# A two-layer graph kernel: the first batch's epilogue by halves and in another order, and the last head's columns finished as a half and two quarters

## The chip, the cores and the metric

The kernel runs on one core of one Trainium2 chip. The time is the device time of the whole program in microseconds (us), the median of several executions. All data is float32. The engines are called PE (TensorE), DVE (VectorE), ACT (ScalarE), POOL (GpSimd) and SP (SyncE, which issues most of the transfers). Each takes its own instructions in program order, and semaphores connect them.

## The reference, cut to what matters

There are 16 graphs (batches) of 1024 nodes with 128 features. Each goes through two layers, and each layer ends in a residual and a layernorm.

```python
# layer 0
h = x @ Ww + Wb
e = (h @ A) @ h.T;  e = e + e.T                        # symmetric scores, 1024 x 1024
attention = softmax(where(adj > 0, e, 0), axis=1) * adj
h_prime = relu(attention @ h)
ic, fc, oc = (sigmoid(h_prime @ w_u + x @ w_x) for three pairs of vectors)
x = layernorm(x + oc * tanh(ic * h_prime + fc * x))
# layer 1, four heads
h = x @ conv_w[head] + conv_b[head]
Ah = tanh(adj * (h @ attn_w[head] @ h.T))
x = layernorm(x + relu(relu(mean over heads of relu(Ah @ h)) + x))
```

## The kernel before

**Tiling.** The 1024 nodes are 8 blocks (`NB`) of 128, or two halves (`NH`) of 512 columns. A matmul works on at most 512 columns; in float32 it is two instructions on PE. PSUM has a ring of four small tiles (`ps_sc`, tag `sc`) that every score, projection and transpose shares, and two accumulators of 1024 columns (`ps_acc`, tags `acc0` for layer 0 and `acc1` for layer 1).

**Layer 0 in pieces.** `layer0(b)` returns a dictionary of pieces with one-letter names, and `run` calls them in the order of a string. For batch b: `L` loads xT and the eight adjacency blocks; `X` loads x; `Q0`, `Q1` project the queries (L199); `H` projects h with the gates' columns, three groups of matmuls (`pR_h`, L268), each followed by a DVE addition (L269); `S0` to `S7` are scores of the upper triangle (L283, copied by ACT into R in L286); `T0` to `T6` turn blocks into the lower triangle, by PE transposes for the first batch (L301), by a DVE transpose and transfers through DRAM for all others (L308 to L315); `A` masks, takes maxima and exponentials (L324 to L330); `B` multiplies by the adjacency and scales h (L335 to L339) and then issues the products of the block before (`back`, L347). After these comes the epilogue: `R` (relu, hpT, L356), `P` and `p` (rows of h', L366), `G` (gates, and POOL's product u = x * gate, L378), `I` (L384 and tanh, L388), `O` (L395), then the layernorm in two steps, `V` (statistics on DVE, L182 to L186, and a power on POOL, L187) and `N` (L190). `turn_x1`, `head_uT` and `rows` then prepare layer 1 (L439, L199, L448).

**Layer 1 in steps.** Each batch has 32 steps (4 heads of 8 blocks). `layer1_step` computes the scores of a block (L469), multiplies by the adjacency on DVE (L470), takes tanh on ACT (L471) and pushes the product with h (`back`, L475) onto a queue that runs two steps later (`DELAY`). When a head is done, `sum` takes its relu (L485, L487). Between the steps stand the pieces of the next batch's layer 0, by the list `BETWEEN`; a piece that has already run is skipped. The queries of the batch after that stand at step 31, its loads at step 28, behind `turn_x1` of step 27 on SP's queue.

**The two ends.** For the first batch the order of pieces is written out by hand, mixed with pieces of the second batch and with `join`, four steps that prepare layer 1's weights:

```python
run(first, "... T5 S6 A5 B4")
run(second, "Q0 Q1")
run(first, "T6 S7 A6 B5 A7 B6 B7")
```

The second batch's S0 to S7 and T0 to T2 all run there. At the other end, `layer1_end` of the last batch transposes the sums on PE (L501), adds x1 (L504, L508), runs the layernorm over all eight blocks and stores 512 KB from POOL's queue (L511).

Of the kernel before, what the change touches and what calls it, by code (L numbers as in the profile page):

```python
# [11 lines left out]
F32 = mybir.dt.float32  # L12
AF = mybir.ActivationFunctionType
ALU = mybir.AluOpType
# [3 lines left out]
P = 128  # L18
# [4 lines left out]
def two_layer_adjacency_kernel(  # L23
# [19 lines left out]
    nc = tc.nc  # L43
# [15 lines left out]
    def small(name):  # L59
        return ps_sc.tile([P, 512], F32, tag="sc", name=name)  # L60
# [108 lines left out]
    def push(back):  # L169
        pending.append(back)  # L170
        if len(pending) > DELAY:
            pending.popleft()()

    def layernorm(t, dst, name):

        st = sb.tile([P, NB, nc.vector.BN_STATS_DIM], F32, tag="st", name=f"st_{name}")
        mv = sb.tile([P, NB, 2], F32, tag="mv", name=f"mv_{name}")  # L180
        for k in range(NB):
            nc.vector.bn_stats(st[:, k, :], t[:, k, :])  # L182
        for k in range(NB):
            nc.vector.bn_aggr(mv[:, k, :], st[:, k, :])
        rs = sb.tile([P, NB], F32, tag="rs", name=f"rs_{name}")
        nc.vector.tensor_scalar_add(rs, mv[:, :, 1], EPS)  # L186
        nc.gpsimd.tensor_tensor(rs, rs, mhalf, ALU.pow)  # L187
        yield
        for k in range(NB):
            nc.vector.tensor_scalar(  # L190
                dst[:, k, :], t[:, k, :], mv[:, k, 0:1], rs[:, k : k + 1],
                ALU.subtract, ALU.mult,
            )
# [41 lines left out]
    def layer0(b):  # L235
# [22 lines left out]
                t["qT"] = sb.tile([P, N], F32, tag="qT0", name=f"qT0_{b}", bufs=1)  # L258
            project_T(t["qT"], q_w, t["xT"], c_col, f"q0_{b}", [q])

        def project_h():

            h = t["h"] = sb.tile([P, NB, G], F32, tag="h0", name=f"h0_{b}", bufs=1)
            for ks in GROUPS:
                ps = small(f"pR_h0_{b}_{ks[0]}")[:, : len(ks) * G]
                ps = ps.rearrange("p (k d) -> p k d", d=G)
                for i, k in enumerate(ks):
                    nc.tensor.matmul(ps[:, i, :], t["xT"][:, ts(k, P)], wwT_g, start=True, stop=True)  # L268
                nc.vector.tensor_add(  # L269
                    h[:, ks[0] : ks[-1] + 1, :], ps,  # L270
                    wb_row.unsqueeze(1).to_broadcast([P, len(ks), G]),
                )
            t["gate"] = sb.tile([P, NB, 3], F32, tag="gate", name=f"gate_{b}")
            nc.vector.tensor_copy(t["gate"], h[:, :, D : D + 3])

        def score(j):
            if j == 0:
# [91 lines left out]
        def gates():  # L369

            gate = t["gate"]
            gflat = gate.rearrange("p k g -> p (k g)")
            nc.vector.tensor_add(gate, t["hp"][:, :, D : D + 3], gate)
            nc.scalar.activation(gflat, gflat, AF.Exp, scale=-1.0)
            nc.vector.tensor_scalar_add(gflat, gflat, 1.0)
            nc.vector.reciprocal(gflat, gflat)
            t["u"] = sb.tile([P, NB, D], F32, tag="u", name=f"u0_{b}", bufs=1)
            nc.gpsimd.tensor_mul(t["u"], t["x"], gate[:, :, 1:2].to_broadcast([P, NB, D]))  # L378

        def inner():  # L380
            u, gate, hp = t["u"], t["gate"], t["hp"]
            for q in range(NH):
                for k in range(q * BH, (q + 1) * BH):
                    nc.vector.scalar_tensor_tensor(  # L384
                        u[:, k, :], hp[:, k, :D], gate[:, k, 0:1], u[:, k, :],
                        op0=ALU.mult, op1=ALU.add,
                    )
                nc.scalar.activation(  # L388
                    u[:, q * BH : (q + 1) * BH, :], u[:, q * BH : (q + 1) * BH, :], AF.Tanh
                )  # L390

        def outer():
            u, gate = t["u"], t["gate"]
            for k in range(NB):
                nc.vector.scalar_tensor_tensor(  # L395
                    u[:, k, :], u[:, k, :], gate[:, k, 2:3], t["x"][:, k, :],
                    op0=ALU.mult, op1=ALU.add,
                )

            t["x1"] = sb.tile([P, NB, D + 1], F32, tag="x1", name=f"x1_{b}")  # L400
            nc.gpsimd.memset(t["x1"][:, :, 0:1], 1.0)
            t["norm"] = layernorm(u, t["x1"][:, :, 1 : D + 1], f"0_{b}")

        def finish():
            next(t["norm"], None)
            x1_t[b] = t["x1"]

        pieces = {
            "L": load, "H": project_h, "X": load_x, "R": relu,
            "P": lambda: rows_hp(GROUPS[:-1]), "p": lambda: rows_hp(GROUPS[-1:]),  # L410
            "G": gates, "I": inner, "O": outer, "V": lambda: next(t["norm"]), "N": finish,
        }
        for q in range(NH):
            pieces[f"Q{q}"] = partial(project_q, q)
        for j in range(NB):
# [39 lines left out]
        project_T(uT, ms[:, hd, :], x1T_t[b], None, f"u1_{b}_{hd}")  # L455
        u_t[b, hd] = uT

    acc1_t, sum_t = {}, {}

    def layer1_step(b, hd, m):  # L460
        x1T, h1, uT = x1T_t[b], h1_t[b, m], u_t[b, hd]
        adj = adj_t[b][m]
        if m == 0:
            acc1_t[b, hd] = ps_acc.tile([P, N], F32, tag="acc1", name=f"acc1_{b}_{hd}")
        acc = acc1_t[b, hd]
        s = sb.tile([P, N], F32, tag="s1", name=f"s1_{b}_{hd}_{m}", bufs=4)
        for q in range(NH):
            ps = ps_sc.tile([P, 512], F32, tag="sc", name=f"sc1_{b}_{hd}_{m}_{q}")
            nc.tensor.matmul(ps, x1T[:, ts(m, P)], uT[:, ts(q, 512)], start=True, stop=True)  # L469
            nc.vector.tensor_mul(s[:, ts(q, 512)], ps, adj[:, ts(q, 512)])  # L470
        nc.scalar.activation(s, s, AF.Tanh)  # L471

        def back():
            for q in range(NH):
                nc.tensor.matmul(  # L475
                    acc[:, ts(q, 512)], h1[:, ts(hd, D)], s[:, ts(q, 512)],
                    start=(m == 0), stop=(m == NB - 1),
                )
            if m == NB - 1:
                if hd == 0:  # L480
                    sum_t[b] = sb.tile([P, N], F32, tag="sum", name=f"sum_{b}", bufs=1)
                for q in range(NH):
                    o, a = sum_t[b][:, ts(q, 512)], acc[:, ts(q, 512)]
                    if hd == 0:
                        nc.vector.tensor_scalar_max(o, a, 0.0)  # L485
                    else:
                        nc.vector.scalar_tensor_tensor(o, a, 0.0, o, op0=ALU.max, op1=ALU.add)  # L487

        push(back)

    def layer1_end(b):
        x1 = x1_t[b][:, :, 1 : D + 1]
        y = sb.tile([P, NB, D], F32, tag="u", name=f"y_{b}", bufs=1)
        if b + 1 < B:
            turn(y.rearrange("p k d -> p (k d)"), sum_t[b].rearrange("p (k d) -> p k d", d=P), f"sum_{b}")
            yield
            nc.vector.scalar_tensor_tensor(y, y, 1.0 / H, x1, op0=ALU.mult, op1=ALU.add)
        for q in range(NH if b + 1 == B else 0):
            pt = small(f"pt2_{b}_{q}")
            for i in range(BH):  # L500
                nc.tensor.transpose(pt[:, ts(i, P)], sum_t[b][:, ts(q * BH + i, P)], ident)  # L501
            rows = slice(q * BH, (q + 1) * BH)

            nc.vector.scalar_tensor_tensor(  # L504
                y[:, rows, :], pt.rearrange("p (k d) -> p k d", d=D), 1.0 / H, x1[:, rows, :],
                op0=ALU.mult, op1=ALU.add,
            )
        nc.vector.scalar_tensor_tensor(y, y, 0.0, x1, op0=ALU.max, op1=ALU.add)  # L508
        yield
        yield from layernorm(y, y, f"1_{b}")  # L510
        nc.gpsimd.dma_start(out[b].rearrange("(k p) d -> p k d", p=P), y)  # L511

# [2 lines left out]
    run(first, "L X")  # L517
    load_late_weights()
    run(second, "L")
    run(first, "Q0 H S0 Q1 T0 S1 A0 T1 S2 A1 B0 T2 S3 A2 B1 T3 S4 A3 B2 T4 S5 A4 B3 T5 S6 A5 B4")  # L520
    run(second, "Q0 Q1")
    run(first, "T6 S7 A6 B5 A7 B6 B7")
    next(join)
    run(first, "R")
    run(second, "H")
    run(first, "P p G")
    next(join)
    run(second, "S0 S1 T0")
    next(join)
    run(first, "I")  # L530
    next(join, None)
    run(second, "S2 S3")
    run(first, "O V")
    run(second, "T1 T2 S4 S5 S6 S7")
    run(first, "N")
    turn_x1(0)
    head_uT(0, 0)
    rows(0, range(NB))

    BETWEEN = [
        "H", "S0", "T0 S1", "T1 S2", "T2 A0", "S3 B0", "T3 A1", "S4 B1",
        "T4 A2", "S5 B2", "T5 A3", "S6 B3", "T6 A4", "S7 B4", "A5", "B5",
        "A6", "B6", "A7", "B7", "X R", "P", "p G", "I",
        "O", "V", "N", "", "", "", "", "",
    ]
    AHEAD = {28: "L", 31: "Q0 Q1"}
    TURN = 27
# [23 lines left out]
        end = layer1_end(b)  # L573
    while pending:
        pending.popleft()()
    for _ in end:
        pass


# [37 lines left out]
```

## Time and profile before

| | us |
|---|---|
| median of 3 runs | 2462.53 |
| lowest and highest | 2461.43, 2468.94 |
| the profiled execution | 2458.88 |
| its span, first to last instruction | 2457.1 |
| PE busy | 2427.1 (99%) |
| DVE busy | 1588.5 (65%) |
| ACT busy | 1083.5 (44%) |

The profile is of one execution. In its rows, an arrow `out<-in` names what an instruction writes and reads, L12 is line 12 of the kernel, and a bracket gives the idle time before an instruction and what ended it. The chain that ended last follows the program back from its last instruction: each piece is what released the next one. The table of stretches gives, for each engine, its busy time in a stretch, and then PE's granted clock, where 1.00 is full speed.

### The profile page before, as it was taken

Reading aid. Unit: us, or ns where it says so; the run is one execution under the profiler, and the core shown is the slowest. Engines: PE = TensorE matmul, PEld = TensorE weight load, DVE = VectorE, ACT = ScalarE, POOL = GpSimd, SP = SyncE. Lnnn points to the kernel's source line nnn. Section 1 sums busy time; section 2 is a strip of 40 time slices with the busy share of each in tenths; the row PEclk is TensorE's granted clock in tenths of the full one; section 3 lists DMA queues with packets and bytes.
Section 4 is the critical chain, followed back from the end, with each engine's and each line's share of the span. In section 5 each row is a group of like instructions: output and inputs, shape, how many; then the busy total and the mean of one; then the engine's idle time right before and its main releaser. Section 6 shows DMA issues by size and latency. Waiting matters only on the chain.

```text
span 2457.1 us, 19849 instructions
## 1 busy us (share of the span) xinstructions
PE 2427.1 (99%) x6159; PEld 1118.7 (46%) x6159; DVE 1588.5 (65%) x3010; ACT 1083.5 (44%) x1522; POOL 112.5 (5%) x91
## 2 busy tenths in 40 slices
PE   8999999999999999999999999999999999999997
PEld 4444444444444444444444444444444444444443
DVE  6665848657576565866658576585765848657554
ACT  5544444444444444434444444344444444444432
POOL 0000000000000000000000000000000000000000
PEclk9999999999999999999999999999999999999999
DMA  5204223041240512314033240322304223051000
GB/s 181 51 11 133 55 95 87 8 145 43 95 94 9 147 34 102 87 26 139 25 116 73 68 109 13 123 67 94 84 11 136 53 94 88 7 148 41 23 21 9
DMA packets 408127, 180.75 MB, mean 74 GB/s; under 512 B 352598, under 2 KB 376022, under 8 KB 408023
## 3 DMA queue, kind: packets, MB, share of 16 engines
q1 hardware_dynamic: 404855, 171.11, 25.1%
q0 software_dynamic: 2304, 8.39, 1.2%
q8 instruction: 49, 0.80, 0.1%
q14 instruction: 55, 0.45, 0.1%
q10 hardware_dynamic: 864, 0.00, 0.0%
HBM read 127.80 MB, written 51.64 MB: 73 GB/s over the span
## 4 chain that ended last, share of the span: by engine, by line
PE 96%; DVE 2%; DMA 1%; SPq 0%; ACT 0%; issue 0%; POOL 0%; POOLq 0%; DVEq 0%; ACTq 0%
PE acc L475 35%; PE sc L469 35%; PE acc L347 9%; PE sc L283 5%; PE pT_u L199 4%; PE pR L448 4%; PE pT_q L199 1%; PE pR_h L268 1%; PE pt L366 1%; DMA xT<-in_xT_dram 1%; SPq L228 0%; POOL rs L187 0%; DVE st L182 0%; DMA dram_x<-turn_x 0%; ACT R L330 0%
## 5 line engine op out<-in xcount | busy, mean ns | idle before, releaser
L470 DVE TENSOR_TENSOR s<-sc,adj 128x512 f32<-128x512 f32 x1024 | 682.4, 685 | 640.0 <-PE sc L469 627.1
L475 PE MATMUL acc<-s,h 128*128 128x512 f32 x2048 | 962.0, 592 | 0.0
L469 PE MATMUL sc<-uT,x1T 128*128 128x512 f32 x2048 | 962.0, 592 | 0.0
L471 ACT ACTIVATE s<-s 128x1024 f32<-128x1024 f32 x512 | 541.5, 1058 | 824.9 <-DVE s L470 820.0
L475 PEld LDWEIGHTS acc<-s,h 128*128 128x128 f32 x2048 | 387.7, 190 | 491.2 <-issue 482.1
L469 PEld LDWEIGHTS sc<-uT,x1T 128*128 128x128 f32 x2048 | 385.7, 190 | 468.8 <-issue 423.3
L347 PE MATMUL acc<-R,hz 128*128 128x512 f32 x512 | 243.0, 597 | 4.4 <-ACT hz L339 4.4
L330 ACT ACTIVATE R<-R,nmax 128x1024 f32<-128x1024 f32 x128 | 147.0, 1149 | 207.8 <-DVE nmax L328 196.9
L335 DVE TENSOR_TENSOR R<-R,adj 128x1024 f32<-128x1024 f32 x128 | 156.1, 1219 | 5.4 <-ACT R L330 0.2
L328 DVE TENSOR_REDUCE nmax<-R 128x1 f32<-128x1024 f32 x128 | 156.1, 1220 | 4.4
L324 DVE SCALAR_TENSOR_TENSOR R<-adj,R 128x1024 f32<-128x1024 f32 (+1 forms) x129 | 153.0, 1187 | 3.9 <-PE turn L301 3.9
L347 PEld LDWEIGHTS acc<-R,hz 128*128 128x128 f32 x512 | 95.9, 191 | 113.7 <-issue 87.2
L283 PE MATMUL sc<-xT,qT 128*128 128x512 f32 (+3 forms) x384 | 143.9, 486 | 0.0
L286 ACT ACTIVATE R<-sc,h 128x512 f32<-128x512 f32 (+1 forms) x192 | 108.8, 578 | 38.8 <-PE sc L283 37.2
L199 PE MATMUL pT_u<-x1T,ms 128*128 128x512 f32 x256 | 120.4, 592 | 0.0
L187 POOL TENSOR_TENSOR rs<-rs,mhalf 128x8 f32<-128x8 f32 x32 | 64.6, 2018 | 1211.8 <-DVE rs L186 758.7
L448 PE MATMUL pR<-cw,x1T 128*128 128x512 f32 x256 | 114.9, 592 | 0.0
L339 ACT ACTIVATE hz<-h,rz 128x128 f32<-128x128 f32 x128 | 51.2, 400 | 128.3 <-DVE rz L337 128.1
L283 PEld LDWEIGHTS sc<-xT,qT 128*128 128x128 f32 x384 | 69.7, 190 | 68.8 <-issue 57.0
L451 ACT COPY h<-pR 128x512 f32<-128x512 f32 x128 | 74.9, 585 | 41.9 <-PE pR L448 41.9
L487 DVE SCALAR_TENSOR_TENSOR sum<-acc,sum 128x512 f32<-128x512 f32 x96 | 61.8, 686 | 35.9 <-PE acc L475 35.1
L308 DVE STREAM_TRANSPOSE turn<-R 128x896 f32<-128x896 f32 (+6 forms) x105 | 73.2, 697 | 14.1 <-DMA dram<-turn 11.4
(96 smaller groups left out, 909.4 us busy)
## 6 DMA issues: line engine op xcount, KB each, us to landing
adj<-in_adjT_dram SPq DMA_DIRECT2D x128, 512.0 KB, 7.7
xT<-in_xT_dram SPq DMA_DIRECT2D x16, 512.0 KB, 4.5
x<-in_x_dram SPq DMA_DIRECT2D x16, 512.0 KB, 4.1
out_dram<-y POOLq DMA_DIRECT2D x16, 512.0 KB, 4.0
dram_x<-turn_x SPq DMA_DIRECT2D x15, 512.0 KB, 2.6
x1T<-dram_x SPq DMA_DIRECT2D x60, 128.0 KB, 3.2
dram_sum<-turn_sum SPq DMA_DIRECT2D x15, 512.0 KB, 2.6
y<-dram_sum SPq DMA_DIRECT2D x60, 128.0 KB, 3.1
```

What stands on the lines that cost most here:

```text
L199: nc.tensor.matmul(ps, w, src[:, ts(q, 512)], start=True, stop=True)
L283: nc.tensor.matmul(ps[:, : at - lo], t["qT"][:, ts(j, P)], t["xT"][:, lo:at], start=True, stop=True)
L324: nc.vector.scalar_tensor_tensor(s[:, ks], adj[:, ks], 0.0, s[:, ks], op0=ALU.is_gt, op1=ALU.mult)
L328: nc.vector.tensor_reduce(nmax, s, AX.XY, ALU.max, negate=True)
L330: nc.scalar.activation(s, s, AF.Exp, bias=nmax, accum_out=t["z", j])
L335: nc.vector.tensor_mul(s, s, adj_t[b][j].rearrange("p (k d) -> p k d", d=P))
L347: nc.tensor.matmul(t["acc"][:, ts(q, 512)], t["hz", j], t["R"][:, ts(q, BH), j, :], start=(j == 0), stop=(j == NB - 1),)
L448: nc.tensor.matmul(ps, x1T_t[b][:, ts(k, P)], cw.rearrange("p h d -> p (h d)"), start=True, stop=True)
L469: nc.tensor.matmul(ps, x1T[:, ts(m, P)], uT[:, ts(q, 512)], start=True, stop=True)
L470: nc.vector.tensor_mul(s[:, ts(q, 512)], ps, adj[:, ts(q, 512)])
L471: nc.scalar.activation(s, s, AF.Tanh)
L475: nc.tensor.matmul(acc[:, ts(q, 512)], h1[:, ts(hd, D)], s[:, ts(q, 512)], start=(m == 0), stop=(m == NB - 1),)
```

## The change

In the opening, `H` is divided into its three groups, `H0`, `H1` and `H2`. For the first batch, u, `I`, `O`, `V` and `N` work on two halves of four blocks (`PARTS`); the other batches keep one part. The memset of x1's first column moves from `O` to `G` for all batches. The written order is new: T6 and S7 stand ahead of the second batch's Q0 and Q1, the first batch's `P p G` ahead of the second batch's `H0 H1`, T0 to T2 of the second batch come after the first batch's epilogue, and its S4 to S7 are left to the list `BETWEEN`.

At the end, the last head's tanh results are all kept in one tile (in the buffer of R). Its queue runs the products of columns 0 to 511 alone. Columns 512 to 767 and 768 to 1023 follow as two quarters, each in a PSUM tile of its own (`last_back`), and `last_end` finishes four, two and two blocks with a store from SP each.

```diff
-        st = sb.tile([P, NB, nc.vector.BN_STATS_DIM], F32, tag="st", name=f"st_{name}")
...
+        n = t.shape[1]
+        st = sb.tile([P, n, nc.vector.BN_STATS_DIM], F32, tag="st", name=f"st_{name}")
...
-        nc.gpsimd.tensor_tensor(rs, rs, mhalf, ALU.pow)
+        nc.gpsimd.tensor_tensor(rs, rs, mhalf[:, :n], ALU.pow)
...
-            nc.gpsimd.tensor_mul(t["u"], t["x"], gate[:, :, 1:2].to_broadcast([P, NB, D]))
+            t["x1"] = sb.tile([P, NB, D + 1], F32, tag="x1", name=f"x1_{b}")
+            for ks in PARTS:
+                nc.gpsimd.tensor_mul(
+                    t["u"][:, ks], t["x"][:, ks],
+                    gate[:, ks, 1:2].to_broadcast([P, ks.stop - ks.start, D]),
+                )
+            nc.gpsimd.memset(t["x1"][:, :, 0:1], 1.0)
...
+        PARTS = [slice(0, NB)] if b else [slice(0, BH), slice(BH, NB)]
...
+        last = (b, hd) == (B - 1, H - 1)
+        if last:
+            if m == 0:
+                kept.append(sb.tile([P, NB, N], F32, tag="R", name="kept", bufs=1))
+            s = kept[0][:, m, :]
...
-        push(back)
+        push(partial(back, [0]) if last else back)
...
+    def last_back(acc, ms, at):
+
+        for m in ms:
+            nc.tensor.matmul(
+                acc, h1_t[B - 1, m][:, ts(H - 1, D)], kept[0][:, m, at : at + 256],
+                start=(m == 0), stop=(m == NB - 1),
+            )
+        if ms[-1] == NB - 1:
+            add_head(B - 1, H - 1, acc, at)
...
+    def last_end(b, k0, k1):
+
+        n = k1 - k0
+        x1 = x1_t[b][:, k0:k1, 1 : D + 1]
+        y = sb.tile([P, n, D], F32, tag="s1", name=f"y_{b}_{k0}", bufs=4)
+        pt = small(f"pt2_{b}_{k0}")[:, : n * P]
+        for i in range(n):
+            nc.tensor.transpose(pt[:, ts(i, P)], sum_t[b][:, ts(k0 + i, P)], ident)
+        nc.vector.scalar_tensor_tensor(
+            y, pt.rearrange("p (k d) -> p k d", d=D), 1.0 / H, x1, op0=ALU.mult, op1=ALU.add
+        )
+        nc.vector.scalar_tensor_tensor(y, y, 0.0, x1, op0=ALU.max, op1=ALU.add)
+        yield from layernorm(y, y, f"1_{b}_{k0}")
+        rows = out[b, k0 * P : k1 * P, :]
+        nc.sync.dma_start(rows.rearrange("(k p) d -> p k d", p=P), y)
...
-    run(first, "Q0 H S0 Q1 T0 S1 A0 T1 S2 A1 B0 T2 S3 A2 B1 T3 S4 A3 B2 T4 S5 A4 B3 T5 S6 A5 B4")
-    run(second, "Q0 Q1")
-    run(first, "T6 S7 A6 B5 A7 B6 B7")
+    run(first, "Q0 H0 S0 H1 H2 Q1 T0 S1 A0 T1 S2 A1 B0 T2 S3 A2 B1 T3 S4 A3 B2 T4 S5 A4 B3")
+    run(first, "T5 S6 A5 B4 T6 S7 A6 B5")
+    run(second, "Q0")
+    run(first, "A7 B6")
+    run(second, "Q1")
+    run(first, "B7 R")
     next(join)
-    run(first, "R")
-    run(second, "H")
     run(first, "P p G")
+    run(second, "H0 H1")
     next(join)
-    run(second, "S0 S1 T0")
+    run(second, "S0")
+    run(first, "I0 I1")
+    run(second, "S1")
+    run(first, "O0 V0 O1")
     next(join)
-    run(first, "I")
+    run(second, "H2 S2")
+    run(first, "V1")
     next(join, None)
-    run(second, "S2 S3")
-    run(first, "O V")
-    run(second, "T1 T2 S4 S5 S6 S7")
-    run(first, "N")
+    run(second, "S3")
+    run(first, "N0 N1")
     turn_x1(0)
     head_uT(0, 0)
+    run(second, "T0 T1 T2")
     rows(0, range(NB))
...
-    for _ in end:
-        pass
+    ends = [last_end(B - 1, k, k + n) for k, n in ((0, 4), (4, 2), (6, 2))]
+    for i, at in enumerate((512, 768)):
+        acc = ps_acc.tile([P, N], F32, tag=f"acc{i}", name=f"acc_end_{i}")[:, :256]
+        last_back(acc, range(NB // 2), at)
+        next(ends[i])
+        if i:
+            next(ends[i - 1], None)
+        last_back(acc, range(NB // 2, NB), at)
+    next(ends[2])
+    for e in ends[1:]:
+        next(e, None)
```

## Prediction

> **What bounds the kernel now.** Read the page first: engine shares, then its chain that ended last.
>
> ```profile
> span 2457.1 us, 19849 instructions
> PE 2427.1 (99%) x6159; PEld 1118.7 (46%) x6159; DVE 1588.5 (65%) x3010; ACT 1083.5 (44%) x1522; POOL 112.5 (5%) x91
> PE 96%; DVE 2%; DMA 1%; SPq 0%; ACT 0%; issue 0%; POOL 0%; POOLq 0%; DVEq 0%; ACTq 0%
> ```
>
> PE is the bound. From 69.9 us to 2440.3 its matmuls follow each other at 0.43 us per 512-column instruction, bar some 4 us. So time can be won only before that stretch, where PE starves, and after it, where PE is done and other engines finish. The chain over the first 130 us comes next (columns: start, length, what):
>
> ```profile
> 41.77 3.57 PE acc L347 x4
> 45.35 2.01 PE acc L347 x4
> 47.36 1.05 PE p_last L145 x2
> 48.41 1.92 PE acc L347 x4
> 50.33 1.80 PE pR_h L268 x16
> 52.12 1.79 PE pt L366 x16
> ...
> 56.83 0.59 DVE turn L308
> ...
> 57.86 2.14 DVE u L384 x8
> 60.01 2.10 DVE u L395 x8
> 62.11 1.55 DVE st L182 x8
> ...
> 64.49 1.69 POOL rs L187
> ```
>
> After the first batch's last products (acc) the chain passes through work of the second batch (pR_h, turn) before the first batch's gates and layernorm. The timeline and the table of stretches show what made acc late:
>
> ```profile
> 37.60 1.22 DVE L324 SCALAR_TENSOR_TENSOR R<-adj,R 128x1024 f32<-128x1024 f32 x1 [0.75 <-PE turn L301]
> 38.60:42.00 3.40, 1.13 (x4) 0.30 (x3) 3.37 (x5) 2.46 (x6) 0.00 (x0) 1.00 1.03 418
> 42.00:45.40 3.40, 3.39 (x5) 0.79 (x4) 3.20 (x5) 1.54 (x3) 0.00 (x0) 0.50 0.45 178
> ```
>
> DVE waited 0.75 for a transpose that stood behind the second batch's Q0 Q1 on PE; PE then had 1.13 us of work in 3.4 us, and its granted clock was 0.50 for the next 3.4. Last, the chain of the end:
>
> ```profile
> 2435.31 5.17 PE acc L475 x12
> 2440.47 0.02 issue
> 2440.49 0.70 DVE sum L487
> ...
> 2447.06 1.66 POOL rs L187
> 2448.72 2.74 issue
> 2451.46 0.96 POOLq L613
> ```
>
> After PE's last product at 2440.3 come 16.8 us of adding, transposing, layernorm and store in one block.
>
> **The change, part 1: the opening.** Times are in this profile's clock.
>
> *H0 S0 H1 H2.* Between 7.84 and 17.3 us PE has no gap and the same instructions stand before Q1; T0 starts at 14.87 either way, and A0's mask waits for T0. I take 0; ends 0 and 0.5 gained, as S0's copies on ACT start a microsecond earlier.
>
> *T6 S7 ahead of the second batch's Q0, Q1.* A6's mask starts at 36.77, when DVE is free, not 37.60: 0.83 earlier, and everything paced by DVE (masks, maxima, products, 3.6 us per column block) with it. The last hz, at 46.36 before, starts at 45.53 and ends 45.93. On PE, Q0 now lies between back(4) and back(5), Q1 between back(5) and back(6): in 38.6 to 42.0 PE has about 0.5+0.86+1.0 = 2.4 us of work, and 2.4 in the next stretch. The stretches 62.5 to 65.9 and 65.9 to 69.3 hold 2.33 and 2.59 and the clock stays at 1.00, so I expect no half clock. Then back(5) runs 40.94-42.66, Q1 to 43.5, back(6) 44.5-46.2, back(7) 46.2-48.0, and hpT starts at 48.2, against 50.36. Here the Trainium skill speaks against me: "TensorE: Matmul & The Clock Gate", Part 1, says that the clock falls only after an idle window of about 3.4 us. The gap here was 2.4 us (39.3 to 41.77), so by the rule it was not what halved the clock, and the half clock would stay: back(5), Q1, back(6) would end at about 47.0, and 0.65 us be lost. The trace has the clock falling right behind that one stretch, and I go by it.
>
> *H of the second batch moved behind P p.* Before, pt began at 51.96 behind 1.80 us of pR_h. Now it follows p_last (1.05 us) at 49.0: 2.96 earlier. hp, gates and reciprocal keep their 3.4 us: they end at 52.39 (55.35 before).
>
> *T0 moved behind the epilogue; u in two halves.* POOL's product took 1.91; two halves of about 1.0 leave the first ready at 53.5. DVE meanwhile adds two groups of h (0.61 and 0.49, to 53.5), and its 1.11 us transpose is gone from here. So the eight u instructions (L384, 0.2625 each) run 53.55-55.65, against 57.86-60.0. ACT must first finish S0's two copies (to 55.2), then tanh twice (0.63 each). O0 starts at 55.9 (59.93 before).
>
> *Layernorm by halves.* Four u instructions to 56.95, four statistics (0.193 each), four aggregates and eps: the first POOL power starts at 58.36. DVE goes on with O1 (1.05), the moved third h group and gate copy (0.6), statistics and aggregates: the second power starts at 61.35 (the only one before: 64.49). Its width is 4 columns where the trace has only 8, at 1.66. POOL's memsets of 1 to 8 columns take 0.09 to 0.11, so the fixed part is small and the power's own work large. Ends: 0.88 (0.1 fixed, the rest by columns) and 1.66 (no saving). I take 1.14, nearer the first. The first half's four x1 instructions run beside it, from 61.15. The second half starts at 62.53, PE's last transpose follows 1.17 later as before (68.00 to 68.40 for the last one), and pT_u starts at 63.86, against 68.56: 4.70 gained, 3.9 to 5.0 with the ends.
>
> *The bill.* Before, the second batch's S4 to S7 filled PE's idle time; now they run inside batch 0's dense stretch, where each PE instruction costs its time: 2x(0.429+0.322+0.216+0.11) = 2.15 us. Their ACT copies (2.1 us) and the three DVE transposes (2.5 us, now at 64.5-67) stand beside PE, on engines under 65% busy; if DVE were not free, the first masks of batch 0 (about 73 us) would be next to wait. SP's transfers for these tiles move with them, some 8 us, and are first needed around step 6, near 97 us. Net: 4.70 - 2.15 = 2.55.
>
> **Part 2: the end.** Call T the end of PE's last score matmul: 2435.14 before, but 4.29 earlier now, since five of the eight products of the last head have lost their second half (5x0.86). PE: back(5), back(6) to T+1.72; back(7) waits for tanh, which ended 2.05 after the scores (2437.19): 0.4 idle, then to T+2.96. The kept scores lie in the buffer of R, free since step 20 of the batch before: 0. The first quarter's four products to 4.67 (eight 256-column instructions), four transposes to 5.15, the other four to 6.87, the second quarter to 8.59, two transposes, to 10.59. The Trainium skill ("TensorE: Matmul & The Clock Gate", Back-to-back issue gap) says that spacing is set by the weight load and the matmul together, and gives 81 ns where 56 is the bare value at 128 columns. At 25 ns each the 32 quarter instructions would cost 0.8 more. But the 256-column row of this trace (L283) steps at 0.216, exactly half of 0.429, and the 132-column row (L268) at 0.112, each with its load of 0.19 beside the one before; I take 0.
>
> DVE: the half's add waits for T+3.16, done 3.85, hidden behind PE. y 5.36-6.01, max 6.70, statistics, aggregates, eps to 8.1; add of quarter one to 8.5; y, max and statistics of rows 4-5 from 9.05 to 10.7; normalising the half (four of 0.257) to 11.75. Only now can the last quarter's add run, whose sums were ready at 10.8: the new wait, 1 us, caused by DVE's order. Then add 12.15, transposes, y 12.67, max, statistics, eps 14.35; power on 2 columns 14.48 to 15.36 (ends 0.49 and 1.66; I take 0.88); two normalisations to 16.0. The store goes out on SP: 128 KB, for which the DMA table's row dram<-turn of that size gives 2.0 (before: 512 KB from POOL, 0.6 of waiting and 3.9 to land). The two stores before it leave at 11.8 and 15.0, on a queue with nothing else left. Landed at 18.0, and the 1.7 us of closing semaphores after it stay: end at T+19.7. Before, with this T, the end was at 21.95+4.29 = 26.2. Gain 6.5; with the ends of the power 5.7 to 6.9.
>
> **Sum.** 2.55+6.5 = 9.05 against this execution's 2458.88 (span 2457.1 and 1.8 around it): 2449.8. This execution lies 3.65 below the median of the three runs; from that median, 2462.53, I get 2453.5, or -0.37%. Epilogues of later batches keep their order; only POOL's 0.10 us memset comes before the power there, and POOL is 5% busy.
>
> **The rivals.**
>
> *The gain shrinks to within 0.3%.* 0.3% is 7.4 us, about what a measurement of this kernel can tell from no change. It takes 1.65 us off my sum: both powers at their full 1.66 (0.8 in the tail, 0.5 in the opening) and the clock halving after all (0.65): 7.1 left, 2455.4. With the weight load exposed (0.8) and about 1.3 lost to dependencies coarser than I assume (the sum at 2440.49 waited for both halves), 5 are left: 2457.5. For it: no trace of a narrow power, four places with new waits. Against: those are four misses in one direction.
>
> *Slower.* At each batch boundary pT_q needs xT, which SP issues only after turn_x1's write and four reads have gone: at 199.6 us, landing 4.1 to 5.9 later, and PE starts pT_q at 204.33. There is almost no margin, and the waits show PE held there by xT three times, 2.1 us in all, 1.0 at most. If the new alignment made each of the 14 boundaries wait 0.9 longer, 12.6 are lost: 3.5 slower, 2466. It decides at 9.05/14 = 0.65 us per boundary. Against: SP's order and the steps from 24 to 31 of each batch are unchanged. For: the runs shown spread over 7.5 us, and it is a wait of this kind that could do so.
>
> *The halves don't separate.* If the half's add still waited for everything, the tail would start at PE's end, T+10.6 against T+9.4 before; the store gives 2.5 back, the opening 2.55: 4 gained in all, 2458.5. It is part of the within case; the half and the quarters have tiles of their own, which speaks against it.
>
> **How the numbers follow.** Forecast 0.77, gain within 0.3% 0.17, slower 0.06; these are the three chances. The likeliest time is 2453.5. Unknown powers give +-1.3, the spread of medians some 3; low end 2449.5, high end 2459.5, which takes in the shrunken gain.
>
> **What would show it.** Right: no stretch at clock 0.50 near 42 us; hpT near 48.2; the first pT_u of layer 1 near 63.9; S4 to S7 of the second batch after 90 us; one 0.4 us PE gap before the last back, 256-column products stepping at 0.216, the last add on DVE behind four normalisations, a last store of about 2 us. Wrong: a first pT_u later than 66.4 (the opening then gains nothing net), a gap in PE between 70 us and the last head, or more than 20.5 us from the last score to the end.

## The result, and the profile after

| | before | after |
|---|---|---|
| median, us | 2462.11 (6 runs) | 2453.21 (6 runs) |
| lowest and highest | 2461.23, 2468.94 | 2452.39, 2454.80 |
| ratio, 95% interval | | 0.9959 (0.9946 to 0.9972) |
| the profiled execution | 2458.88 | 2454.80 |
| its span | 2457.1 | 2453.0 |

The change saves 8.9 us between the medians; 9.05 were forecast. The two profiled executions, however, differ by only 4.1: before's was 3.2 below its median, after's 1.6 above. Both numbers have to be explained. First the same three lines of the page, of the changed kernel:

```profile
span 2453.0 us, 19886 instructions
PE 2428.0 (99%) x6175; PEld 1121.2 (46%) x6175; DVE 1590.2 (65%) x3017; ACT 1082.8 (44%) x1522; POOL 112.9 (5%) x94
PE 92%; DVE 3%; DMA 2%; SPq 1%; POOL 0%; issue 0%; ACT 0%; POOLq 0%; DVEq 0%; ACTq 0%
```

PE's busy time is the same. What is new is in the last line: PE's part of the chain fell from 96% to 92%, DMA rose from 1% to 2% and SPq from 0% to 1%. In this execution the chain runs back through transfers of xT at batch boundaries. The chain of waits through the opening, after (start, length, what):

```profile
45.48 3.70 PE acc L351 x8
49.18 1.05 PE p_last L145 x2
50.23 1.55 PE pt L370 x12
...
53.74 1.05 POOL u L384
54.80 0.02 issue
54.82 2.96 DVE u L394 x8
57.78 1.05 DVE u L405 x4
58.83 0.78 DVE st L183 x4
...
63.02 1.05 POOL rs L188
```

The second batch's pR_h and transpose have left the chain: p_last is followed by pt at once. The last eight acc instructions now take 3.70 us in one run. Before, the same eight took 2.01 and 1.92, with p_last between them; the four ahead of these took 3.57, at half clock, and have left the chain too. And one line is longer than it should be: eight u instructions of L394 in 2.96 us, against 2.14 before. The two stretches that were at 1.13 us of PE work and then at half clock:

```profile
38.60:42.00 3.40, 2.66 (x7) 0.88 (x6) 3.37 (x5) 1.78 (x5) 0.00 (x0) 1.00 1.02 414
42.00:45.40 3.40, 2.74 (x6) 0.95 (x6) 3.20 (x5) 1.94 (x5) 0.00 (x0) 1.00 0.41 165
```

PE now has 2.66 and 2.74 us of work in them (the second number), where about 2.4 were reckoned, and the granted clock (third from the right) is 1.00 in both. Then the end, in the timeline after:

```profile
2435.41 1.12 PE L500 MATMUL acc<-kept,h 128*128 128x512 f32 x2 [0.16 <-ACT kept L496]
2436.37 1.89 PE L523 MATMUL acc_end<-kept,h 128*128 128x256 f32 x8
...
2444.28 1.11 DVE L191 TENSOR_SCALAR y<-y,mv,rs 128x128 f32<-128x128 f32 x4
2444.51 0.70 POOL L188 TENSOR_TENSOR rs<-rs,mhalf 128x2 f32<-128x2 f32 x1 [1.71 <-DVE rs L187]
2445.30 0.42 DVE L518 SCALAR_TENSOR_TENSOR sum<-acc_end,sum 128x256 f32<-128x256 f32 x1
```

The last add (last row) starts as the four normalisations (row of L191) end. Its sums had left PE at about 2444.2, so nothing else held it. This is the wait of 1 us that the prediction had named.

**Where the time is, by three marks.** I cut each trace at the start of layer 1's first pT_u and at T, the end of PE's last score matmul (its start and one step of 0.43). "xT waits" are summed over the 14 pT_q at the batch boundaries: by how much each starts later than one step of 0.43 after the matmul before it. They lie inside the middle stretch. "Full clock from" is the first moment at which the granted clock is 1.00; PE's first matmul is at 3.0 to 3.3 in every trace. The last five rows are experiments, told below.

| kernel | full clock from | first pT_u | pT_u to T | of it xT waits | T to the end |
|---|---|---|---|---|---|
| before | 11.30 | 68.56 | 2366.58 | 2.91 | 21.92 |
| after | 13.07 | 65.44 | 2367.94 | 6.08 | 19.66 |
| after_again | 11.26 | 64.51 | 2364.02 | 2.43 | 19.63 |
| after_x | 13.97 | 65.78 | 2361.14 | 0 | 19.63 |
| s47_x | 11.57 | 65.21 | 2359.00 | 0 | 19.63 |
| sum_first_x | 11.36 | 64.55 | 2360.93 | 0 | 18.70 |
| both_x | 13.05 | 65.92 | 2358.79 | 0 | 18.70 |

In the new end T comes 4.29 earlier, because ten product instructions of the last head (0.429 each) now lie behind it. So, of the pair after and before: opening 3.12 won; middle stretch 2366.58 - 2.91 - 4.29 = 2359.38 before and 2367.94 - 6.08 = 2361.86 after, 2.48 lost; xT waits 3.17 lost; end 21.92 + 4.29 - 19.66 = 6.55 won. Together 4.02, the difference of the spans.

### The profile page after: what moved, and what is told of

It is laid out like the page before. It is cut to its first block, busy times and chain, and to the rows that moved or that the text cites. A ratio compares the mean times of both kernels' runs of the same rounds, so it can differ in the third digit from the quotient of the medians.

```text
span 2453.0 us, 19886 instructions
## 1 busy us (share of the span) xinstructions
PE 2428.0 (99%) x6175; PEld 1121.2 (46%) x6175; DVE 1590.2 (65%) x3017; ACT 1082.8 (44%) x1522; POOL 112.9 (5%) x94
## 4 chain that ended last, share of the span: by engine, by line
PE 92%; DVE 3%; DMA 2%; SPq 1%; POOL 0%; issue 0%; ACT 0%; POOLq 0%; DVEq 0%; ACTq 0%
PE sc L494 33%; PE acc L500 33%; PE acc L351 9%; PE sc L287 5%; PE pT_u L200 4%; PE pR L465 4%; DMA xT<-in_xT_dram 2%; PE pT_q L200 1%; PE pt L370 1%; PE pR_h L271 1%; SPq L229 1%; DMA dram_x<-turn_x 1%; DVE x L191 0%; DVE st L183 0%; POOL rs L188 0%
## 5 line engine op out<-in xcount | busy, mean ns | idle before, releaser
L495 DVE TENSOR_TENSOR s<-sc,adj 128x512 f32<-128x512 f32 x1008 | 671.3, 685 | 625.6 <-PE sc L494 613.8
L500 PE MATMUL acc<-s,h 128*128 128x512 f32 x2016 | 947.4, 592 | 0.0
L496 ACT ACTIVATE s<-s 128x1024 f32<-128x1024 f32 x504 | 532.9, 1057 | 806.0 <-DVE s L495 799.6
L500 PEld LDWEIGHTS acc<-s,h 128*128 128x128 f32 x2016 | 381.7, 190 | 483.7 <-issue 474.4
L339 DVE TENSOR_TENSOR R<-R,adj 128x1024 f32<-128x1024 f32 x128 | 156.2, 1220 | 5.4 <-ACT R L334 0.2
L188 POOL TENSOR_TENSOR rs<-rs,mhalf 128x8 f32<-128x8 f32 (+2 forms) x35 | 65.8, 1880 | 1212.4 <-DVE rs L187 886.7
```

The source lines that it names most:

```text
L339: nc.vector.tensor_mul(s, s, adj_t[b][j].rearrange("p (k d) -> p k d", d=P))
L500: nc.tensor.matmul(acc[:, ts(q, 512)], h1[:, ts(hd, D)], s[:, ts(q, 512)], start=(m == 0), stop=(m == NB - 1),)
```

## The experiments

**The two parts apart.** open_only has the new opening and the old end, end_only the old opening and the new end.

```diff
# open_only
-        last = (b, hd) == (B - 1, H - 1)
+        last = False
...
# end_only
-        PARTS = [slice(0, NB)] if b else [slice(0, BH), slice(BH, NB)]
+        PARTS = [slice(0, NB)]
...
+    run(second, "Q0 Q1")
+    run(first, "T6 S7 A6 B5 A7 B6 B7")
```

> The opening of the changed kernel with the end of the kernel before. Theory (the opening gives about 2 net, the end about 6.5): 2460 us, the first pT_u near 65 us in the trace (68.6 before), 22 us from the last score matmul to the end, no stretch at half clock near 42 us. Rival (the moved S4 to S7 eat the opening's whole gain, all of it came from the end): 2462, with the first pT_u near 66.4. A rival for the rest: if the waits at the batch boundaries had grown because of the new opening, 2464 or more.

> The opening order of the kernel before with the end of the changed kernel. Theory: 6.5 less than before, 2455.6 us; 19.6 us from the last score matmul to the end, against 22.0 with a last score that is 4.3 earlier; first pT_u at 68.6, and the half clock near 42 us back. Rival (the two parts depend on each other, or the end gives under 5): 2457.5 or more.

| | median | lowest, highest | ratio, 95% interval |
|---|---|---|---|
| before, same chip | 2459.99 (26 runs) | 2457.33, 2463.58 | |
| open_only | 2458.01 (13 runs) | 2456.86, 2458.94 | 0.9992 (0.9984 to 1.0000) |
| end_only | 2454.06 (6 runs) | 2450.67, 2459.53 | 0.9971 (0.9959 to 0.9983) |

The opening alone gives 2.0, with an interval that reaches no gain at all, and the end alone 5.9. The two add up to 7.9, near the 8.9 of both, which is from another set of runs. In open_only's trace the first pT_u starts at 65.75 and no stretch near 42 is at half clock, as expected; end_only came with the half clock, but its first pT_u was expected at 68.6. What the medians hide is the spread: end_only's six runs lie 8.9 us apart and open_only's thirteen only 2.1. The spread goes with the old opening. The trace of end_only, at 2459.53 its slowest run, shows it in the table of stretches:

```profile
40.85:44.26 3.41, 1.32 (x3) 0.68 (x4) 3.38 (x5) 1.54 (x3) 0.00 (x0) 1.00 1.02 412
44.26:47.68 3.42, 2.34 (x4) 0.65 (x3) 3.07 (x5) 1.70 (x4) 0.00 (x0) 0.50 0.03 12
...
71.57:74.98 3.41, 1.59 (x7) 0.98 (x7) 3.23 (x10) 1.10 (x3) 1.26 (x1) 1.00 0.41 134
74.98:78.40 3.42, 3.42 (x6) 1.61 (x6) 0.03 (x1) 1.19 (x3) 0.00 (x0) 0.50 0.67 108
```

PE has 1.32 us of work in one stretch of 3.41, and the clock is 0.50 in the next (third number from the right); in this run it stayed there until 57.92, four stretches. The same happens a second time, behind the stretch in which PE waits 1.86 for the first batch's normalisation. The first pT_u starts at 75.34, against 68.56 in the trace of before, with the same opening.

**Is it the waits for xT?** In after's trace the xT waits had doubled, which is what the slower rival foretold. The waits in the trace of before, then in two traces of the changed kernel, its first one and that of after_again, which is the changed kernel once more in a later set of runs (engine, line, waited for: total, times, longest). This view counts from the modelled end of the matmul before, so its totals are smaller than those of the table:

```profile
PE pT_q L199 <- DMA xT<-in_xT_dram: 2.1, 3, 1.0
```

```profile
PE pT_q L200 <- DMA xT<-in_xT_dram: 4.5, 7, 1.1
```

```profile
PE pT_q L200 <- DMA xT<-in_xT_dram: 1.6, 4, 0.5
```

> The changed kernel once more, beside the others of this set. Theory (the waits for xT at the boundaries are a chance of each execution, and the same for all kernels with this load order): 2450.5 to 2453.5 us, waits of 2 to 6 us in the trace. Rival (the change itself lengthens these waits): 2453 or more, 5.5 us of waits or more, as in the first trace.

after_again took 2450.61 us (2449.70 to 2452.00, 5 runs) against 2461.85 of before on that chip (2457.78 to 2468.00, 11 runs): ratio 0.9954 (0.9941 to 0.9967). Its waits are below those of before. The same program waits 6.08 in one execution and 2.43 in another, so the longer waits of the first trace are not a cost of the change; what makes them vary was not looked into. To see what the waits are worth, the xT transfer leaves load `L` and goes out at step 20 rather than step 28, ahead of the transfers of turn_x1, in both kernels:

```diff
-    AHEAD = {28: "L", 31: "Q0 Q1"}
+    AHEAD = {20: "l", 28: "L", 31: "Q0 Q1"}
```

> The kernel before, with one transfer moved: the next but one batch's xT is issued behind x at step 20, not behind the turning of x1 at step 28. Theory (pT_q at the boundaries waits for xT, and this wait is what spreads the runs): no wait at the boundaries in the trace (2.9 us in the one of before), 2457 to 2459 us, lowest and highest within 1.5 us. Rival (the spread has another source): 2461 to 2462.5 and a spread of 4 to 7 us as before.

> The changed kernel with the same transfer of xT moved to step 20. Theory: the 6.1 us of waits at the boundaries that its trace shows are gone, 2447 to 2448.5 us, lowest and highest within 1.5 us. Rival (what the early xT gives is lost again, by colliding with other transfers): 2452 to 2454.

| | median | lowest, highest | ratio, 95% interval |
|---|---|---|---|
| before_x | 2457.72 (13 runs) | 2455.12, 2459.47 | 0.9987 (0.9979 to 0.9995) |
| after_x | 2447.45 (5 runs) | 2447.13, 2448.36 | 0.9948 (0.9936 to 0.9961) |

The waits are gone in both traces (0 at all 14 boundaries), and both kernels gain: before 2.3 on the same chip, the changed kernel 3.2 against after_again's median from another chip (2.9 in the middle stretches of the two traces). The gap between before_x and after_x is now 10.3. The expectation for before_x failed in one point: without the waits its runs were to lie within 1.5 us, and they lie 4.4 apart. So the waits are not the main source of the spread, which the slower rival of the prediction had thought possible. after_x's runs do lie within 1.2 us: with the new opening and no xT waits little chance is left, so the following edits are made on after_x. They ran on other chips than after_x itself, and the medians of before on the chips used lie between 2458.38 and 2463.77. Differences of 1 or 2 us against after_x are therefore carried by the marks in the table above, taken inside each trace, and not by the medians or the intervals of the ratios.

**Parts of the opening.** end_only_x is end_only with the early xT. q_first_x only puts the second batch's Q0 Q1 ahead of T6 S7 again. t_first_x is end_only_x with only that one move of the new opening (T6 S7 first, Q0 and Q1 between the last products). The lines below are cut from their differences to the changed kernel.

```diff
# q_first_x
-    run(first, "T5 S6 A5 B4 T6 S7 A6 B5")
-    run(second, "Q0")
-    run(first, "A7 B6")
-    run(second, "Q1")
-    run(first, "B7 R")
+    run(first, "T5 S6 A5 B4")
+    run(second, "Q0 Q1")
+    run(first, "T6 S7 A6 B5 A7 B6 B7 R")
...
# t_first_x
-        PARTS = [slice(0, NB)] if b else [slice(0, BH), slice(BH, NB)]
+        PARTS = [slice(0, NB)]
...
+    run(second, "S0 S1 T0")
+    run(first, "I0")
+    run(second, "S2 S3")
+    run(first, "O0 V0")
+    run(second, "T1 T2 S4 S5 S6 S7")
+    run(first, "N0")
```

> The opening order of the kernel before, the changed end, and xT early, so that no boundary waits blur it. Theory (what the old order costs is mostly that PE starves near 42 us and its clock is halved for one to four stretches of 3.4 us, as chance has it): lowest run about 2449, median about 2451.5, highest over 2454, with a lower mean clock in the longer runs. Rival (the opening's gain is the order of work alone, 1.5 to 2 us): all runs within 1.5 us, about 2449.5, against 2447.5 for the changed kernel with xT early.

> The changed kernel with xT early and the second batch's Q0 and Q1 both ahead of T6 and S7 again, nothing else undone. Theory (this order is what starves PE): the mask of A6 waits 0.8 for its transpose again, the half clock comes back in the trace near 42 to 58 us, lowest run 2448.3, highest over 2451. Rival (the half clock came from the other parts of the old opening, or from chance): 2448.3 in all runs within 1.5 us, clock 1.00 from 14 us on.

> The opening of the kernel before with this one edit (T6 and S7 first, then Q0 and Q1 one by one between the last products), the changed end, and xT early. Theory: the half clock is gone, runs within 1.5 us of each other at about 2449, and what is left to the changed kernel's 2447.5 is the rest of the opening (1 to 2 us). Rival: spread and median like those of the old opening.

| | median | lowest, highest | ratio, 95% interval | stretches at half clock in its trace |
|---|---|---|---|---|
| end_only_x | 2453.02 (6 runs) | 2448.45, 2456.76 | 0.9961 (0.9947 to 0.9975) | 43.65 to 50.47, 70.95 to 74.36 |
| q_first_x | 2448.61 (5 runs) | 2447.74, 2449.20 | 0.9945 (0.9930 to 0.9959) | 42.97 to 46.38 |
| t_first_x | 2448.96 (5 runs) | 2447.69, 2449.55 | 0.9945 (0.9932 to 0.9958) | 66.79 to 70.20 |
| after_x | 2447.45 (5 runs) | 2447.13, 2448.36 | 0.9948 (0.9936 to 0.9961) | none |

Each of the two risky places comes back with its own part of the old order: the stretch near 43 with Q0 Q1 ahead, the one near 67 with the rest. In t_first_x's trace PE waits 1.85 there for the normalisation of the undivided layernorm (PE pt, waiting for DVE x L191). But t_first_x brings back the order of the second batch's pieces as well, so that it is the undivided layernorm was not shown by an edit of its own. Two expectations failed: q_first_x was to show runs beyond 2451, but it costs 1.2 at the median and its runs stay within 1.5 us; and t_first_x was to be without half clock. Moving T6 S7 alone (t_first_x) brings end_only_x's median down by 4.1, on the same chip.

The best run of end_only_x, 2448.45, is only 1.3 above after_x's best, which is about what the order of the work itself is worth. The rest, at the median, is half-clock stretches that no longer occur. The mean granted clock of each run says so too: in end_only_x it falls from 0.998 in the two shortest runs to 0.996 in the longest, and all runs of after_x have 0.999. Of the 55 runs of before made beside the experiments, 30 have 0.997, with a median of 2459.0, and six have 0.994, with 2466.7.

**Halving u.** The 2.96 us in the chain. The one line of L394, after (duration in ns, lowest, median, highest):

```profile
L394 DVE SCALAR_TENSOR_TENSOR u<-hp,gate,u x8: 339/339/1117, 54.8 to 57.4; 128x128 f32<-128x128 f32 x8
```

One of eight took 1117 ns. In the trace it is the first, from 54.819 to 55.936, while POOL's second half of x * gate ran from 54.743 to 55.788. u_whole_x makes POOL's product one instruction again:

```diff
-            for ks in PARTS:
+            for ks in [slice(0, NB)]:
```

> Edit on after_x: POOL's product u = x * gate of the first batch is one instruction of 1024 columns again, instead of two of 512; everything else stays. Theory (contention): in the changed kernel the first DVE instruction of u (two inputs in SBUF) took 1.117 us, against 0.339 for its fellows, because POOL's second half of the product ran beside it, so halving gained almost nothing. Then with one product (1.9 us) DVE's first u instruction starts about 0.9 later but takes 0.34, and O0 starts as late after the gates' reciprocal as in the changed kernel, 4.35 us, within 0.15; the time stays at after_x's 2447.5, within 0.5. Rival (the halving gives the earlier start that was reckoned): O0 starts 0.9 later, 5.2 after the reciprocal, and the time is 2448.4.

The same line in u_whole_x:

```profile
L398 DVE SCALAR_TENSOR_TENSOR u<-hp,gate,u x8: 344/347/353, 56.1 to 58.0; 128x128 f32<-128x128 f32 x8
```

The long instruction is gone, and DVE starts later. O0's first instruction comes 4.44 after the gates' reciprocal starts (58.23 - 53.79), against 4.35 in after_x (58.05 - 53.70): halving gains 0.09 of the 0.9 that it should. The times, 2447.96 (2447.32 to 2448.51, 5 runs; ratio 0.9935, 0.9922 to 0.9948) and 2447.45, overlap. So the second half on POOL is what held DVE up. The Trainium skill ("SBUF — State Buffer", SBUF: two separate sides) has the rule that fits: DVE and GpSimd share a pair of ports under an exclusive lock, and a DVE instruction with two SBUF inputs waits for the whole of a GpSimd instruction that reads SBUF. The trace agrees nearly: POOL's second half had 0.97 to go when DVE started, DVE lost 0.78 of it, and its instruction ended 0.15 after POOL's. The prediction should have applied it. But another place of the same trace doesn't fit "the whole of": POOL's power on 4 columns, from 60.17 to 61.24, reads SBUF as well, and three of the u instructions of L405, with both tensors in SBUF, start beside it; all eight of L405 take 341 to 347 ns. Why that power doesn't hold them up is open.

**The wait of the last add.** sum_first_x puts the last quarter's add ahead of the half's normalisations, which it splits in two pairs (and gives the statistics a third buffer, not shown):

```diff
+            if split and k == n // 2:
+                yield
...
+        last_back(acc, range(NB // 2, NB), at)
         next(ends[i])
         if i:
             next(ends[i - 1], None)
-        last_back(acc, range(NB // 2, NB), at)
```

> Edit on after_x: at the end, the last quarter's add on DVE stands ahead of the half's four normalisations (the half's statistics tiles get a third buffer, and its normalisation is split: two blocks after that add, two later, beside the last power on POOL). Theory: the 1 us that the last add waits behind four normalisations is on the path of the end; the add starts at T+10.9 instead of T+11.9 (T is the end of PE's last score matmul), the program ends at T+18.6 instead of T+19.6, and the time is 1.0 below after_x: 2446.4. Rival (another bound takes its place: the half's store, now later, becomes the last to land, or the last rows' work waits for the half's normalisation anyway): T+19.6, 2447.5 or above.

2446.35 us (2446.00 to 2446.88, 5 runs), ratio 0.9929 (0.9914 to 0.9944); on this chip, which also ran u_whole_x and s47_x, before took 2463.77 (2457.80 to 2467.74, 9 runs). The timeline of DVE, and below it that of SP:

```profile
2436.37 0.42 DVE L524 SCALAR_TENSOR_TENSOR sum<-acc_end,sum 128x256 f32<-128x256 f32 x1
2436.70 0.59 DVE L193 TENSOR_SCALAR y<-y,mv,rs 128x128 f32<-128x128 f32 x2
...
2439.12 1.62 DVE L193 TENSOR_SCALAR y<-y,mv,rs 128x128 f32<-128x128 f32 x6
```

```profile
2439.75 1.48 SPq L562 DMA_DIRECT2D out_dram<-y  x3
```

The add runs at T+10.9 rather than T+11.9, and the end comes at T+18.7 rather than T+19.6. Six normalisations and three stores now stand at the very end, in 1.6 and 1.5 us. They were the risk; next to the T+18.6 expected they cost about 0.1.

**The bill.** s47_x brings the second batch's S4 to S7 back into the opening:

```diff
-    run(second, "S3")
+    run(second, "S3 S4 S5 S6 S7")
```

> Edit on after_x: the second batch's S4 to S7 are back in the opening, right after its S3 and ahead of the first batch's N0 N1, instead of between layer 1's steps. Theory (the bill): in the dense stretch these pieces cost PE 2.15 us; in the opening PE has idle time for most of them, so the first pT_u comes up to 1.3 later but 2.15 less is left for the dense stretch: 0.9 faster than after_x, 2446.6. Rival (no bill: the dense stretch has holes that absorb them, or ACT's four copies in the opening delay the first batch's x1): the first pT_u is 1.3 or more later and nothing comes back: 2448.8.

2446.22 us (2445.81 to 2446.66, 5 runs), ratio 0.9928 (0.9915 to 0.9941): 1.2 below after_x's median. In the table of marks the middle stretch shrinks from 2361.14 to 2359.00, by 2.14; 2.15 was the bill. The first pT_u comes at 65.21, 0.66 later than in sum_first_x, whose clock warmed up 0.2 earlier: some 0.55 for what four scores cost in the opening, where up to 1.3 was expected.

**Both.** both_x has the last two edits together.

> Edit on after_x: both edits that helped, S4 to S7 of the second batch in the opening again, and the last quarter's add ahead of the half's normalisation. Theory (they lie in different places and add up): 1.23 and 1.10 below after_x's 2447.45 give 2445.1, within 0.6; the stretch from the first pT_u to the last score is 2359.0, the end after it 18.7. Rival (one undoes the other's gain, or its gain was chance of the clock): 2446.3 or above.

2445.30 us (2445.00 to 2445.62, 5 runs) on a chip on which before took 2458.38 (2457.44 to 2462.64, 9 runs): ratio 0.9942 (0.9928 to 0.9956). The marks are 2358.79 and 18.70, as the sum of the two parts says. This is the fastest version: 2.2 below after_x, and 7.9 below the changed kernel's median (2453.21), though these come from other sets of runs.

## Why the prediction was right, and where not

**The end, forecast 6.5, measured 6.55.** Step by step, from T:

| step | forecast | trace of after |
|---|---|---|
| PE idle before the last product of the half | 0.4 | 0.32 |
| the half's add starts | 3.16 | 3.20 |
| the first quarter's add starts | 8.1 | 8.15 |
| the last add starts, after four normalisations | 11.75 | 11.93 |
| power on 2 columns | 0.88 | 0.70 |
| the last store | 2.0 | 1.83 |
| the program ends | 19.7 | 19.66 |

PE's idle time is counted in steps of 0.43 here, as the forecast did; the 0.16 in the timeline row, earlier, counts from the modelled end. The 256-column products step at (1.89 - 0.379)/7 = 0.216, as the score rows had said, so the 0.8 that the prediction worked out from the skill's section on the back-to-back gap did not come. The low ends of the powers rested on a fixed part of 0.1, read from the memsets; it is about 0.38 (see the last section). Errors of 0.2 in both directions cancelled.

**The opening, forecast 2.55, measured about 1.9.** after's clock warmed up 1.8 us later than before's, by chance, and its first pT_u comes 0.93 later than after_again's. Compared like with like (after_again, 11.26 against 11.30), the first pT_u starts at 64.51: 4.05 gained, 4.70 forecast. The bill was right: 2364.02 - 2.43 - 2359.38 = 2.2 in that trace, 2.14 by s47_x, 2.15 forecast. after_again's rows show where 0.65 went. hpT starts at 48.3 (48.2 forecast), the reciprocal ends at 52.7 (52.4), O0 starts at 56.8 (55.9). The step that failed is "two halves of about 1.0 leave the first ready at 53.5 ... the eight u instructions run 53.55-55.65": the start was nearly right (53.9, and 0.3 of the delay was inherited), but the first of the eight waited for POOL's second half. A part of it came back from the power on 4 columns, mean 1.05, forecast 1.14.

**The half clock.** The rule of the skill that the prediction names would have kept the half-clock stretch in place, at a cost of 0.65; I went by the trace. All eight traces with T6 S7 ahead and the layernorm by halves are without one. Here the trace was the better guide, but I under-rated what it showed: I took one execution's single stretch for the whole cost, where other executions of the same order had three (end_only_x) and five (end_only).

**The sum.** 8.9 against 9.05 is closer than its parts, and that closeness is luck. The opening's order gave 0.65 less than reckoned. The xT waits, which I had left alone, were 3.2 longer in the profiled pair. Against that, before's profiled execution was 3.2 below its median and after's 1.6 above: 4.1 + 3.2 + 1.6 = 8.9. The prediction reckoned its gain in that one execution and took it from the median, as if slower executions would stay as much slower after the change. The granted clocks of the runs, above, say that slower executions of before spend more time at half clock; which stretches those are no trace of a slow run of before shows.

**The rivals.** Slower, by xT waits: the place was right (7 waits in place of 3), the cause was wrong, since after_again (2.43), open_only (3.42) and end_only (2.06) lie around the 2.91 of before. Halves that don't separate: the half's add starts at T+3.20, with the quarters still to run, so they do. The shrunken gain needed both powers at 1.66 and the half clock to stay; neither occurred. That H0 S0 H1 H2 in the other order costs nothing was not tried by itself.

## What to carry to other kernels

Where a new order feeds PE in a starved stretch, its worth is not only the microseconds moved: it can also remove half-clock stretches that come and go from run to run, and a smaller spread of the runs is the first sign of it. Cut a trace at two or three marks and compare the pieces of several executions, since the pair of profiles alone (4.1) told less than half of the gain. When a product on POOL is split so that DVE can start on its first half, look at what POOL does next: here its second half, which reads SBUF, held up a DVE instruction with two inputs in SBUF, and the split gained 0.09 of 0.9.

## What the hardware showed that I had not expected

**A fixed grid and a threshold.** In every trace the clock changes only at multiples of 3.41 us from the moment when it first became full. I laid that grid over 14 traces and read PE's busy time in each cell up to 80 us. Behind the eight cells with 1.14 to 1.59 us of work (a third to 47%) the next cell ran at 0.50; behind cells with 1.65 us or more, at full clock, it never did. Two cells of before_x stand on either side:

```profile
41.42:44.83 3.41, 1.65 (x4) 0.68 (x4) 3.38 (x5) 1.54 (x3) 0.00 (x0) 1.00 0.91 370
...
65.31:68.73 3.42, 1.54 (x8) 0.99 (x6) 3.19 (x13) 1.49 (x4) 1.68 (x1) 1.00 0.68 176
68.73:72.14 3.41, 3.41 (x9) 2.02 (x9) 1.00 (x4) 1.29 (x3) 0.00 (x0) 0.50 0.35 56
```

The first was followed by a cell at 1.00, the second by the third row, at 0.50. The Trainium skill ("TensorE: Matmul & The Clock Gate", Part 1) has the free-running window, and the grid agrees with its 3.4 us; that the clock falls only after an idle window does not agree, since PE was busy for up to 1.59 us of these. The ends of the programs, which lie outside these 80 us, fit the same line: a cell of after_again with 1.62 us was followed by 0.50, one of end_only with 1.80 by 1.00. Only PE's busy time was compared; whether the length of a single gap counts as well was not separated from it. With the old order a gap of PE lies near the threshold, and how the grid falls decides: before_x's own gap near 42 passed at 1.65, before's at 1.14 did not. The new order keeps 2.15 us or more in each cell, in eight traces. In seven other half-clock cells PE was busy for 2.99 us or more, and the next was at 1.00. Why end_only stayed at 0.50 behind two cells in which PE was busy throughout remains open.

**The power's size.** The line of L188, after:

```profile
L188 POOL TENSOR_TENSOR rs<-rs,mhalf x35: 697/1667/2480, 60.2 to 2448.3; 128x8 f32<-128x8 f32 x30, 128x4 f32<-128x4 f32 x3, 128x2 f32<-128x2 f32 x2
```

2 columns take 0.70, 4 columns 1.03 to 1.07, 8 columns mostly 1.67: about 0.38 and 0.16 a column, so a narrow power has a fixed part, and on 2 columns it still costs less than half of the wide one.

**The shared ports, the other way round.** The 2480 ns are the same power on 8 columns. In before's trace 14 of its 32 powers take 2.48, in after's 14 of 35, and they are just those at whose start DVE's product of L335 (L339 after), with both inputs in SBUF, was 0.23 into its 1.22. The others on 8 columns take 1.68 or less, most of them beside a DVE product that reads PSUM as well. So the waiting seen in the opening also goes the other way, and costs POOL 0.81 once in each batch but the first and the last; this was read from the traces, not tried by an edit. It is hidden there, behind PE.
